# A four-layer graph network on one core: upper target classes in pairs of source blocks, and a third tile picked from SBUF in layer 2

## The chip, the cores and the metric

The kernel runs on one core of one Trainium2 chip. The metric is the device time of one execution in microseconds; before the change it is 7265.93 us, the median of three runs from 7258.8 to 7266.82. Five engines work side by side, each with its own instruction queue: TensorE (PE) multiplies matrices, VectorE (DVE) and ScalarE (ACT) do elementwise work, GpSimd (POOL) here mostly issues gathers, and SyncE (SP) issues most plain transfers. TensorE's weight loads are a row of their own, PEld. SBUF is the working memory of 128 partitions, PSUM holds what TensorE writes, and DRAM holds inputs, outputs and the tables between layers.

## The reference, cut to what matters

There are 12500 nodes with 128 features and 200000 edges, each with a source and a target (src, dst). Targets are sorted and crowd at low numbers: dst is 12500 u^2 for a uniform u. Each of four layers normalizes the nodes, computes messages along the edges, sums them at nodes, and adds the result to x. Layer 0 is a graph attention and layer 1 an attention with eight heads. The two layers that the change concerns most are these, cut to their sums:

```python
# layer 2: every edge counts in both directions
row = concat([src, dst]); col = concat([dst, src])
deg = segment_sum(ones, row) + 1;  dinv = rsqrt(deg)
xw = h @ W
y = segment_sum(dinv[row] * dinv[col] * xw[col], row) + dinv**2 * xw + b
# layer 3: the sums go to the targets only
neigh_sum = segment_sum(feature[src], dst);  deg = segment_sum(1, dst)
h = feature @ W_self.T + neigh_sum / max(deg, 1) @ W_neigh.T + b   # then batch norm, relu, residual
```

So layer 2 needs two kinds of sums: at each edge's source, of rows that belong to its target, and at each edge's target, of rows that belong to its source. Layer 3 needs the second kind only.

## The kernel before, in words

Nodes are held in 98 blocks (NB) of 128 lanes. In layer 0's background the edges are sorted by source block and, inside a block, by target; that order serves layers 1 to 3.

**Sums at the sources (sum_rows, layer 2).** The sorted edges are laid out in 16 tiles (TB) of 128 edges for each source block, and 56 more tiles hold what does not fit. For each tile a gather (an indirect DMA from POOL, line 355) fetches the 128 rows of the edges' targets from the table zt, a 0/1 matrix (hot) says which lane each edge belongs to, and two matmuls (a row is stored as two halves of 16 bits, PARTS) add the rows up in PSUM (line 1988). Four tiles are a group; there are 406 groups, and a row buffer holds a group, in six buffers. As edges of a block are sorted by target, the first tile of a block only points to targets 0 to 127, and the second to 18 to 273. These two are not gathered in blocks 0 to 96: the rows of WINDOWS lie in SBUF (near_rows), the edges' targets are loaded (targets, line 1948), a compare makes a 0/1 matrix of them (line 1951), three matmuls pick the rows (line 1956), and ACT copies them into the row buffer (line 1958). Layer 1 does the same for its own table with the same WINDOWS. The choice depends on the data, so a test made with the lists (source_tiles) sets a flag, and a slow path that gathers everything stands behind it.

**Sums at the targets (buckets, layers 2 and 3).** Targets are cut into 32 classes (CLASSES): 16 (FEW) below target 4864 (SPLIT), 20 to 500 targets wide, and 16 above, 480 wide each. A bucket is one class and one source block; it has room for 128 edges, and a flag (over) sends the work to a slow path if one holds more. A pass handles four classes (AT_ONCE), and goes over all 98 blocks. A load brings two blocks of rows (z, line 962) and their buckets' lane numbers (lanes, line 964, 256 KB, spread to all partitions); DVE compares the lanes (mine, line 968, 512 wide); then, two buckets at a time, which is called a step here, PE reads each bucket's rows out of the block (pout, line 975), DVE makes a 0/1 matrix of places in the class (yours, line 977), ACT copies what was read to SBUF (r, line 980), and PE adds it to the class's sums (line 951, two matmuls per bucket). Layer 2 has 8 passes (all classes); layer 3 has 4, since it sums targets from SPLIT on by late gathers (late_sums).

**What sets the order.** In layer 2, sum_rows walks through the 406 groups and takes steps of the buckets between them; bucket_shares gives each step a cost by its columns, so that a group gets its share of the steps and the two end together. When four classes are done, finish and layer2_out work off the blocks that are complete and store their rows for layer 3 (h). The framework's scheduler then places the instructions; SP's queue is one, and its loads wait in it for their buffers in order. z and lanes have three buffers each, mine two, yours four, pout two.

**The lists of buckets (bucket_starts).** In layer 1's background, written by hand into its order (manual_schedule), the beginnings of all buckets are found: the 3136 keys in 25 columns of 128 (BC) are compared with the first edge of every row of edges (125 compares of 320, line 855), and two gathers per column (bedge) fetch the row that a bucket begins in and then the 128 edges from there. From these come the lanes and the places in the class, stored to DRAM.

Of the kernel before, what the change touches and what calls it, by code (L numbers as in the profile page):

```python
# [79 lines left out]
CLASSES = 2 * FEW  # L80
CURVE, BEND, STEEP, FLAT = 20, 13, 494, 480


def bound(k):

    if k < BEND:
        return CURVE * k * k
    return CURVE * BEND ** 2 + STEEP * (k - BEND) if k < FEW else SPLIT + FLAT * (k - FEW)
# [9 lines left out]
BUCKETS = NB * CLASSES  # L98
BC = -(-BUCKETS // P)
# [5 lines left out]
NEAR, LOW = 2, 18  # L105
WINDOWS = ((0, 0), (1, LOW + P), (1, LOW))

# [25 lines left out]
class Net:  # L133
# [674 lines left out]
    def bucket_starts(self, work, take, keys, firsts, shifted, lanes, places, over):  # L808
# [8 lines left out]
        nc.vector.tensor_scalar(k, k, CLASSES - 1, None, op0=OP.bitwise_and)  # L817
# [3 lines left out]
        k, low, mid, top = (work.tile([P, 2], F32, name=f"bb{i}") for i in range(4))  # L821
# [3 lines left out]
        nc.vector.tensor_scalar(top, k, float(FLAT), float(SPLIT - FLAT * FEW), op0=OP.mult, op1=OP.add)  # L825
        nc.vector.tensor_sub(top, top, mid)
        nc.vector.tensor_sub(mid, mid, low)
        nc.vector.scalar_tensor_tensor(mid, k, BEND - 0.5, mid, op0=OP.is_ge, op1=OP.mult)
        nc.vector.scalar_tensor_tensor(top, k, FEW - 0.5, top, op0=OP.is_ge, op1=OP.mult)
        nc.vector.tensor_add(bound, low, mid)  # L830
        nc.vector.tensor_add(bound, bound, top)
        yield
        cols = work.tile([P, 2], I32, name="bcols")
        nc.vector.tensor_copy(cols, bound)
        nc.vector.tensor_scalar(cols, cols, 7, KEY_BITS, op0=OP.logical_shift_left, op1=OP.bitwise_or)
        head = work.tile([P, 1], F32, name="bhead")
        nc.vector.tensor_scalar(head, bound[:, 0:1], -1.0, 1.0, op0=OP.mult, op1=OP.add)
        least, above = (work.tile([P, BC], I32, name=n) for n in ("bleast", "babove"))
        nc.gpsimd.iota(least, pattern=[[P, BC]], base=0, channel_multiplier=1)
        nc.vector.tensor_scalar(least, least, int(math.log2(CLASSES)), 21, op0=OP.logical_shift_right,  # L840
                                op1=OP.logical_shift_left)
        for i, t in ((1, above), (0, least)):
            nc.vector.tensor_tensor(t, least, cols[:, i:i + 1].to_broadcast([P, BC]), op=OP.bitwise_or)
# [4 lines left out]
        counts = work.tile([P, BC, 5], F32, name="bcounts")  # L848
        for h in range(5):
            f = work.tile([P, quarter], F32, name="bfirst", bufs=2)  # L850
# [79 lines left out]
    def bucket_shares(self, passes):  # L930

        costs = []
        for k0 in passes:
            for s in range(NB):
                costs += [PARTS * (2 * D + sum(WIDE[k0 + i:k0 + i + 2])) + 6 * P for i in range(0, AT_ONCE, 2)]
# [1612 lines left out]
```

## Time and profile before

| | |
|---|---|
| median of three runs | 7265.93 us |
| time of the profiled execution | 7251.91 us |
| its span, first to last instruction | 7250.1 us |
| gathers of layer 0 (hw), first to last | 195.5 to 2162.3 us, 1564 of them |
| gathers of layer 1 (kvt), first to last | 2355.1 to 4243.6 us, 1430, and 50 for the buckets' lists |
| gathers of layer 2 (zt), first to last | 4523.7 to 6338.1 us, 1430 |
| late gathers of layer 3 (h) | 6375.9 to 7169.4 us, 596 |
| mean granted TensorE clock | 0.801 |

The layers follow one another, so that each is read as a stage of its own: in a stage, the engine that never waits is the one that sets the end, and the busy share of an engine over the whole span says little. In the lines of the profile, L355 is line 355 of the kernel; out<-in names what an instruction writes and reads; x is a count. A wait is idle time of an engine, with what ended it; "issue" means that nothing in the profile was waited for. A matmul's duration includes its way through the array, and successive matmuls overlap, so what one costs in a row of them is the distance of two starts.

### The profile page before, as it was taken

The numbers are of one execution on the slowest core, as the hardware profiler recorded it, in microseconds if no ns is written. First come the engines' busy times: TensorE is split into PE (matmuls) and PEld (weight loads), VectorE is DVE, ScalarE is ACT, GpSimd is POOL, SyncE is SP. The second block draws the span as 40 slices with busy tenths as digits, with TensorE's granted clock in tenths as the row PEclk, the third lists the DMA queues.
The fourth block names the chain that finished last, engine by engine and source line by source line (L and its number), as shares of the span: only waits on it lengthen the run. The fifth ranks groups of instructions, "written<-read, shape, count | busy, mean of one in ns | idle before, by whom it ended". The sixth has DMA issues, their size and how long they took to land. (4 is left out here: it accounts for less than half of the span.)

```text
span 7250.1 us, 126419 instructions
## 1 busy us (share of the span) xinstructions
PE 5117.9 (71%) x37041; PEld 4050.0 (56%) x37042; DVE 5586.9 (77%) x17921; ACT 3831.6 (53%) x8238; POOL 5039.5 (70%) x5200
## 2 busy tenths in 40 slices
PE   4344544444446777777777753999999998889987
PEld 3334444444433777666677743555565567745675
DVE  5596777777756888767777757888888888988988
ACT  4466666666656443333333326455555556845567
POOL 0777777777762777777777743777777777767774
PEclk7556666666668777777777756999999999989999
DMA  6433333333346766666666641555555555744565
GB/s 109 90 81 81 83 81 82 81 80 82 82 91 198 222 203 205 191 189 194 189 201 197 201 114 51 132 138 137 140 140 137 136 148 161 196 123 121 140 169 160
DMA packets 808143, 1007.00 MB, mean 139 GB/s; under 512 B 201589, under 2 KB 549882, under 8 KB 807162
## 3 DMA queue, kind: packets, MB, share of 16 engines
q1 hardware_dynamic: 578655, 551.06, 26.6%
q0 software_dynamic: 186016, 432.15, 23.4%
q10 hardware_dynamic: 42747, 15.32, 1.0%
q8 instruction: 309, 5.06, 0.3%
q14 instruction: 416, 3.41, 0.2%
HBM read 937.24 MB, written 60.78 MB: 138 GB/s over the span
## 5 line engine op out<-in xcount | busy, mean ns | idle before, releaser
L355 POOL DMA_INDIRECT rows<-hw,idxd x1564 | 1488.8, 952 | 672.9 <-issue 449.6
L980 ACT ACTIVATE r<-pout 128x512 f16<-128x512 f32 x2352 | 1373.3, 596 | 977.8 <-PE pout L975 909.2
L951 PE MATMUL sums<-yours,r 128*128 128x480 f16 (+9 forms) x9408 | 1863.8, 318 | 4.5 <-ACT r L980 3.7
L355 POOL DMA_INDIRECT rows<-zt,idxs x1430 | 1379.8, 965 | 453.3 <-issue 332.6
L355 POOL DMA_INDIRECT rows<-kvt,idxs x1430 | 1390.0, 972 | 435.8 <-issue 348.0
L977 DVE TENSOR_SCALAR yours<-iotac,bucketp 128x480 f16<-128x480 f16 (+8 forms) x4704 | 1356.9, 336 | 207.0 <-PE sums L951 184.8
L1408 PE MATMUL psum<-rows,weights 128*128 128x130 f32 x3128 | 742.4, 418 | 636.2 <-ACT weights L1402 528.2
L951 PEld LDWEIGHTS <-r 128*128 128x128 f16 x9408 | 861.6, 98 | 374.2 <-issue 11.0
L1408 PEld LDWEIGHTS psum<-rows,weights 128*128 128x128 f32 x3128 | 665.5, 314 | 676.1 <-ACT weights L1402 599.4
L975 PE MATMUL pout<-z,mine 128*128 128x256 f16 x4704 | 893.5, 273 | 49.1 <-ACT r L980 26.7
L355 POOL DMA_INDIRECT rows<-h,late x596 | 585.2, 982 | 182.5 <-issue 142.6
L1687 ACT ACTIVATE weighted<-lg 128x64 f32<-128x64 f32 x203 | 53.1, 262 | 1163.0 <-DVE lg L1685 1163.0
L1402 ACT ACTIVATE weights<-off,weight,minus 128x128 f32<-128x128 bf16 x1173 | 483.3, 481 | 334.7 <-DVE minus L1392 187.0
L975 PEld LDWEIGHTS <-mine 128*128 128x128 f16 x4704 | 431.3, 97 | 325.7 <-issue 72.8
L1708 PE MATMUL psum<-weighted,hot 128*128 128x137 f32 x3136 | 557.8, 347 | 64.8 <-DVE weighted L1697 64.4
L1708 PEld LDWEIGHTS psum<-weighted,hot 128*128 128x128 f32 x3136 | 530.3, 252 | 81.8 <-DVE weighted L1697 76.7
L1681 DVE TENSOR_TENSOR rows<-pq,rows 128x512 f32<-128x512 f32 x406 | 278.7, 687 | 307.3 <-DMA rows<-kvt,idxs 306.2
L1668 PE MATMUL pq<-query,mine 128*128 128x128 f16 x3136 | 296.7, 270 | 262.2 <-DVE mine L1637 239.5
L1661 PE MATMUL pb<-we,near 128*128 128x16 f32 x3248 | 448.3, 281 | 9.7 <-ACT near L1630 9.7
L1661 PEld LDWEIGHTS pb<-we,near 128*128 128x128 f32 x3248 | 441.3, 218 | 22.1 <-ACT near L1630 11.4
L968 DVE TENSOR_SCALAR mine<-lanes,lane 128x512 f16<-128x512 f16 x1176 | 426.4, 365 | 17.4 <-PE pout L975 15.6
L1668 PEld LDWEIGHTS <-mine 128*128 128x128 f16 x3248 | 274.3, 127 | 288.4 <-DVE mine L1637 263.1
(525 smaller groups left out, 9074.7 us busy)
## 6 DMA issues: line engine op xcount, KB each, us to landing
lanes<-lanes SPq DMA_DIRECT2D x588, 256.0 KB
near<-lengths SPq DMA_DIRECT2D x203, 512.0 KB
lanes<-slanest SPq DMA_DIRECT2D x203, 256.0 KB
z<-zt SPq DMA_DIRECT2D x392, 128.0 KB
lanes<-dlanes SPq DMA_DIRECT2D x195, 256.0 KB
z<-h SPq DMA_DIRECT2D x196, 128.0 KB
rows<-hw,idxd POOLq DMA_INDIRECT x1564
rows<-kvt,idxs POOLq DMA_INDIRECT x1430
```

The source lines that it names most:

```text
L355: self.nc.gpsimd.indirect_dma_start(out=out, out_offset=None, in_=table, in_offset=bass.IndirectOffsetOnAxis(ap=idx[:, t:t + 1], axis=0))
L951: nc.tensor.matmul(sums[i], self.part(r[:, i, :], h), yours[i], start=s == NB - 1 and h == 0, stop=s == 0 and h == PARTS - 1)
L968: nc.vector.tensor_scalar(mine, lane[:, s - first, :], self.lane, None, op0=OP.is_equal)
L975: nc.tensor.matmul(p[:, j, :], mine[:, (i + j) * P:(i + j + 1) * P], z[:, s - first, :], start=True, stop=True)
L977: nc.vector.tensor_scalar(yours[j], self.iotac[:, :wide[i + j]], place[:, b:b + 1], None, op0=OP.is_equal)
L980: nc.scalar.activation(r, p, AF.Copy)
L1402: nc.scalar.activation(hot[:, j, :], off, AF.Relu, bias=w[:, j:j + 1], scale=minus[:, j:j + 1])
L1408: nc.tensor.matmul(p, hot[:, j, :], rows[:, j, :n], start=j % G == 0, stop=j % G == G - 1)
L1661: nc.tensor.matmul(pb[:, j].rearrange("p a h -> p (a h)"), s["near"][:, j * P:(j + 1) * P], self.we.rearrange("p a h -> p (a h)"), start=F ...
L1668: nc.tensor.matmul(pq[:, j, :], s["mine"][i][:, j, :], s["query"][i * G + j][:, h * D:(h + 1) * D], start=h == 0, stop=h == 1)
L1681: nc.vector.tensor_mul(k, s["pq"][i], k)
L1708: nc.tensor.matmul(p, s["hot"][j // G][:, j % G, :], v[:, j, :], start=first and j == 0, stop=last and j == W - 1)
```

## The change

**Classes.** Below SPLIT everything stays. Above it there are 20 classes (MANY) instead of 16, from 308 targets wide to 460, and a bucket there holds the edges of *two* source blocks, 64 lanes (HALF) for each. A pass over upper classes goes over 49 pairs; each load of z brings a pair, its lanes are half as large, and a bucket is read by two matmuls of 64 lanes, each writing half of the partitions. There are five upper passes and four lower ones. z and lanes have two buffers each instead of three.

**Lists.** The keys now are 13 columns of lower buckets and 2 x 8 of the upper ones' halves (SC = 29 for the counting, BC = 21 of buckets), and the edges of an upper column are fetched by two gathers of 64. The compares have one buffer (bfirst) instead of two.

**Third tile.** The third tile's targets are expected from 100 to 611 (NEXT, MORE); its rows are picked by four matmuls, with the compare made against the lane and against the lane plus 256 (further), in a second pout tile and a second copy. This is for layer 2 alone: layer 1 still picks two tiles. source_tiles subtracts 100 from the third tile's targets as it does 18 from the second's, and tests its range.

```diff
-CLASSES = 2 * FEW
-CURVE, BEND, STEEP, FLAT = 20, 13, 494, 480
+MANY = 20
+CLASSES = FEW + MANY
+CURVE, BEND, STEEP = 20, 13, 494
+RISE, SPREAD = 304, 4
 def bound(k):
...
+    return SPLIT + (RISE + SPREAD * (k - FEW)) * (k - FEW)
...
-BUCKETS = NB * CLASSES
-BC = -(-BUCKETS // P)
+HALF = P // 2
+LC = -(-NB * FEW // P)
+TC = -(-NB // 2 * MANY // P)
+SC = LC + 2 * TC
+BC = LC + TC
...
-NEAR, LOW = 2, 18
+NEAR, LOW, NEXT = 2, 18, 100
 WINDOWS = ((0, 0), (1, LOW + P), (1, LOW))
+MORE = ((2, NEXT + P), (2, NEXT), (2, NEXT + 3 * P), (2, NEXT + 2 * P))
...
 def bucket_starts
...
-            f = work.tile([P, quarter], F32, name="bfirst", bufs=2)
+            f = work.tile([P, quarter], F32, name="bfirst")
...
-            for c in range(BC):
+            for c in range(SC):
...
+        def parts(c):
+            if c < LC:
+                return [(slice(0, P), c)]
+            return [(slice(h * HALF, h * HALF + HALF), c + h * TC) for h in range(2)]
+
+        def run(c):
             if c < BC:
                 edges[c] = work.tile([P, P], I32, name="bedge", bufs=4)
-                self.gather(edges[c], table, ri, c)
+                for at, col in parts(c):
+                    self.gather(edges[c][:, at], shifted, ri, col)
...
 def bucket_shares
...
+            two = [sum(WIDE[k0 + i:k0 + i + 2]) for i in range(0, AT_ONCE, 2)]
+            if k0 < FEW:
+                costs += [PARTS * (2 * D + w) + 6 * P for w in two] * NB
+            else:
+                costs += [PARTS * (4 * D + w) + 6 * P for w in two] * (NB // 2)
...
 def buckets
...
-            for s in range(NB - 1, -1, -1):
-                first = s // ZB * ZB
-                if s == first + ZB - 1:
-                    z = work.tile([P, ZB, PARTS * D], STORED, name="z", bufs=3)
+            pairs = k0 >= FEW
+            count = NB // 2 if pairs else NB
+            for s in range(count - 1, -1, -1):
+                first = 2 * s if pairs else s // ZB * ZB
+                if pairs or s == first + ZB - 1:
+                    z = work.tile([P, ZB, PARTS * D], STORED, name="z", bufs=2)
                     nc.sync.dma_start(z, view[:, first:first + ZB, :])
-                    lane = work.tile([P, ZB, n * P], F16, name="lanes", bufs=3)
+                    lane = work.tile([P, ZB, n * P], F16, name="lanes", bufs=2)
+                    if pairs:
+                        at, m = (LC * P + s * MANY + k0 - FEW) * P, n * P
+                    else:
+                        at, m = (k0 // n * (LC * P // FEW) + first) * n * P, ZB * n * P
...
+                        if pairs:
+                            b = LC * P + s * MANY + k0 - FEW + i + j
+                            for h in range(2):
+                                at = slice(h * HALF, h * HALF + HALF)
+                                nc.tensor.matmul(p[at, j, :], mine[:, (i + j) * P + h * HALF:(i + j) * P + (h + 1) * HALF],
+                                                 z[:, h, :], start=True, stop=True)
...
 def sum_rows
...
+        spans = WINDOWS + MORE
+        near_rows = work.tile([P, len(spans), PARTS * D], STORED, name="nearrows")
+        for w, (_, lo) in enumerate(spans):
             nc.sync.dma_start(near_rows[:, w, :], table[lo:lo + P, :])
+        further = work.tile([P, 1], F32, name="further")
+        nc.vector.tensor_scalar_add(further, self.lane, 2.0 * P)
...
+            targets = work.tile([P, 5, P], F16, name="targets")
+            nc.sync.dma_start(targets.rearrange("p w e -> p (w e)"), self.targets_of(tile, 5))
+            chosen = work.tile([P, len(spans), P], F16, name="chosen")
+            nc.vector.tensor_scalar(chosen[:, :5], targets, self.lane, None, op0=OP.is_equal)
+            nc.vector.tensor_scalar(chosen[:, 5:], targets[:, 3:], further, None, op0=OP.is_equal)
+            for tiles in ((0, 1), (2,)):
+                p = psum.tile([P, 2, PARTS * D], F32, name="pout", bufs=2)[:, :len(tiles)]
+                for j, tile in enumerate(tiles):
+                    terms = [w for w, (t, _) in enumerate(spans) if t == tile]
+                    for w in terms:
+                        nc.tensor.matmul(p[:, j, :], chosen[:, w, :], near_rows[:, w, :], start=w == terms[0],
+                                         stop=w == terms[-1])
+                nc.scalar.activation(rows[:, tiles[0]:tiles[-1] + 1, :], p, AF.Copy)
...
-            for j in range(NEAR if close else 0, G):
+            for j in range(3 if close else 0, G):
                 self.gather(rows[:, j, :], table, idx, lo + j)
```

## The prediction

> **What bounds the kernel now.** I read the span by stages first, then what each stage's engines wait for, then a stretch of single instructions. The busy time of each engine in four stretches, each taken from the first gather of a layer to its last (layers 0, 1, 2, 3; the columns after the length are busy us and instructions of PE, weight loads, DVE, ACT, POOL, then clock and DMA):
>
> ```profile
> 195.00:2163.00 1968.00, 892.23 (x5386) 807.60 (x5386) 1416.22 (x3348) 1179.51 (x2917) 1488.64 (x1564) 0.62 0.37 83
> 2355.00:4245.00 1890.00, 1420.87 (x10757) 1347.28 (x10757) 1430.47 (x3727) 718.12 (x1531) 1438.85 (x1481) 0.76 0.65 198
> 4523.00:6340.00 1817.00, 1699.29 (x13154) 1120.54 (x13155) 1540.13 (x6247) 1025.74 (x1831) 1379.77 (x1430) 0.99 0.55 148
> 6370.00:7172.00 802.00, 725.40 (x5966) 504.14 (x5967) 725.77 (x2880) 494.69 (x901) 615.82 (x621) 0.98 0.55 150
> ```
>
> By busy share PE (94%) looks like the limit of layer 2 and POOL (76%) does not. The waits of POOL in layer 2 say otherwise (total us, times, longest us):
>
> ```profile
> POOL rows L355 <- issue: 332.6, 1091, 0.3
> POOL rows L355 <- PE pout L975: 32.0, 105, 0.3
> POOL rows L355 <- DMA rows<-zt,idxs: 22.9, 75, 0.3
> POOL rows L355 <- PE sums L951: 21.0, 69, 0.3
> POOL rows L355 <- DVE hot L1986: 17.7, 1, 17.7
> POOL rows L355 <- PE psum L1988: 13.7, 45, 0.3
> ```
>
> Every wait but the first of the stage is 0.3 us, whoever is named: it is the fixed gap before each gather, not a wait for anybody. The timeline shows the beat, 3.98, 5.23, 6.48:
>
> ```profile
> 5003.98 0.94 POOL L355 DMA_INDIRECT rows<-zt,idxs  x1 [0.30 <-issue]
> 5004.17 0.38 PE L975 MATMUL pout<-z,mine 128*128 128x256 f16 x2
> ...
> 5004.38 0.97 PE L951 MATMUL sums<-yours,r 128*128 128x480 f16 x4
> ...
> 5005.19 0.38 PE L975 MATMUL pout<-z,mine 128*128 128x256 f16 x2
> 5005.23 0.94 POOL L355 DMA_INDIRECT rows<-zt,idxs  x1 [0.30 <-issue]
> ...
> 5005.41 0.97 PE L951 MATMUL sums<-yours,r 128*128 128x480 f16 x4
> ...
> 5006.48 0.94 POOL L355 DMA_INDIRECT rows<-zt,idxs  x1 [0.30 <-PE sums L951]
> ```
>
> So layer 2 is bound by POOL: 1430 gathers from 4523.7 to 6338.1 are 1.270 us each. Layer 1 is too: 1480 gathers (50 of them bedge) from 2355.1 to 4243.6, 1.277 us each. PE is a close second in layer 2. Its step in the upper classes (two bucket reads and four sums) takes 1.02 us when nothing interrupts it (5004.17 to 5005.19 above): four sums of 480 columns at a pitch of 0.20, two reads of 256 columns at 0.11.
>
> **The change, part by part.**
>
> *Third tile (close_rows).* Of the 16 tiles of each of 97 blocks, 14 were gathered and now 13: 97 gathers less, 97 x 1.270 = 123 us off the engine that sets the stage. Added per block: four matmuls of 256 columns (0.11 each by pitch), an eviction of 256 columns (between the 0.27 of the 64-wide and the 0.60 of the 512-wide ACT copy; I take 0.45), one longer and one additional DVE compare (the present 384-wide one takes 0.34; I take 0.42 and 0.30). That is 43 us of PE, 44 of ACT and 37 of DVE, all beside the gathers.
>
> *Upper classes by pairs of blocks.* The steps (two buckets each) go from 8 x 98 x 2 = 1568 to 4 x 98 x 2 + 5 x 49 x 2 = 1274, the upper ones from 784 to 490. An upper step keeps four sums, of 384 columns on average (0.20 x 384/480 = 0.16 each), and has four reads of 64 lanes instead of two of 128. No row shows such a read. Bounds: 0.055 if the two halves run side by side, 0.27 (the whole duration of a read in its row) if each must leave the array before the next enters. I take 0.11, the pitch of the present read, as each half streams the same 256 columns. Step: 4 x 0.16 + 4 x 0.11 = 1.08. PE in the upper classes: 784 x 1.02 = 800 to 490 x 1.08 = 529 us. DVE loses 147 lane compares at 0.365 and 588 of the 1568 compares of 480 columns that take 508.8 us, the others getting narrower (0.30): about 54 + 215 us; ACT loses 294 x 0.596 = 175.
>
> Sum for the stage by engine: PE 1699 - 271 + 43 = 1471, DVE about 1310, ACT 900, POOL's beat 1333 x 1.270 = 1693. POOL stays the bound and PE's cover grows from 7% to 13%. The work per gather group also fits locally: by the planner's costs a group gets 8840 units instead of 11000, so 2.66 upper steps in 1333/406 x 1.27 = 4.17 us. PE needs 2.66 x 1.08 = 2.87, plus 0.65 for eight hot matmuls (pitches of 0.05 to 0.11) and 7 x 0.11/4 = 0.19 for the close ones: 3.7. What is late next is therefore still the gathered rows.
>
> *Mode of the array.* The 64-lane reads use a part of the array, the sums the whole, and they alternate. Layer 0 has such a change already, a 64-column matmul between 128-column ones:
>
> ```profile
> 592.25 0.39 PE L1408 MATMUL psum<-rows,weights 128*128 128x130 f32 x2
> 592.47 0.27 PE L524 MATMUL bank<-ident,keys 128*64 128x128 f32 x1
> 592.58 0.39 PE L1408 MATMUL psum<-rows,weights 128*128 128x130 f32 x2
> ```
>
> Starts 592.25, (592.36), 592.47, 592.58: the same 0.11 pitch into it and out of it, no bubble. [...]
>
> *Bucket lists, in the background of layer 1.* Gathers of edges: 25 + 25 become 29 + 13 + 2 x 8 = 58. Eight more on a bound POOL: 8 x 1.277 = +10 us. (Bounds: 0 if the odd longer intervals of that stage absorb them, 10 if not; the intervals are tight, so 10.) Counting compares 125 to 145 at 0.54 + 0.08: 12 us of DVE, which idles 459 of 1890 us there; the stores of lanes and places go on SP, idle between loads. bfirst has one buffer instead of two, so four times DVE (and behind it that iteration's logits) waits for a 160 KB load, some 3 us. Ten row buffers of four gathers, 50 us of POOL's beat, cover that; without cover 4 x 3 = 12 us.
>
> *Buffers.* z and lanes go from three buffers to two in layers 2 and 3. On SP a z load waits for PE's last read of the old buffer and the lanes load behind it in the queue waits with it. In the trace's DMA records the last packet of a lanes load (256 KB) lands 3.3 us (median) after its issue; before the change it lies 8 to 9 us early in the wide passes, 2.2 us early in the last pass of either layer. With two buffers a load is issued one buffer's time later: 5.2 us in the wide passes (covered), 2.6 in the last one of layer 3, so there about 0.2 to 0.6 us late for 49 loads, +8 to +29; I take 8. In the upper passes of layer 2 a buffer lasts two steps of 4.17/2.66 = 1.57 us, and z has two steps and the sums of a third, 4.3 us, from release to use against some 2.9 (issue 0.37, and z packets that land 1.7 to 2.5 after it); PE's 11% cover stands behind that.
>
> *Small edits.* Four more near-row loads at 0.42 on SP ahead of the first z load and four short DVE operations where the source lists are made: +3.
>
> **Sum** against the profiled execution, 7251.9: -123 + 10 + 8 + 3 = -102, so 7150. That execution is 14 us under the median of the three runs, 7265.9; carried over to the median: **7164 us**.
>
> **Rivals.**
> 1. *PE takes over in the upper classes, but gives back only part.* From a read of (4.17 - 0.84)/2.66 = 1.25, (1.25 - 0.64)/4 = 0.153 us, PE is later than the rows. At 0.18 a group takes 4.45 us, 184 groups lose 53: 7217. For: nearly full PE now, unknown 64-lane reads. Against: the 0.11 pitch at 592.47.
> 2. *The slower one: the half reads serialize.* From 0.207 us a read the 102 us are used up. At 0.27 (fill and stream of each exposed) a step is 1.72, a group 5.42, 184 groups lose 230: 7395. For: weights of 64 lanes just before each read, halves of one bank. Against: the same row in layer 0, and weight loads now overlap (0.10 beside a 0.11 pitch).
> 3. *Late z and lanes.* Were each of the 245 upper loads 0.3 us late beyond PE's cover and layer 3's 196 too: 441 x 0.3 = 132 us, 7296; limited to layer 3 and half of it, 7195. For: SP is one queue in order, and a late z holds the lanes behind it. Against: the 4.3 us above.
> 4. *The guarded fallbacks run*, thousands of us, if a half bucket holds 64 edges or more or a third tile leaves its window. Counted in the inputs: the fullest half holds 62, third tiles reach from 146 to 557 inside 100 to 611. Excluded.
>
> **How the numbers follow.** Forecast 0.69; rival 1 0.10; rival 3 0.07 (of it 0.02 within noise, 0.01 slower); rival 2 0.14, of it 0.01 within noise. A measurement of this kernel tells 0.2%, 15 us, from no change. Faster 0.69 + 0.10 + 0.04 = 0.83, same 0.03, slower 0.14 (rivals 2 and 3). The forecast's own range is 7116 (no new costs and the 20 ns above the 1.25 beat gone) to 7195. To leave out no more than 2 in 10 it goes on to rival 1's end: 7115 to 7255.
>
> **What would show it.** Right: 1333 gathers of zt at 1.26 to 1.28 us, longest wait 0.3; layer 2 about 1690 us from first to last gather; PE waiting for rows more than the 74 us now; 58 bedge gathers and layer 1 10 us longer; layer 3 up to 10 longer. Wrong: POOL waits above 0.3 us for psum or pout (rival 1 and 2), a 64-lane read with a pitch above 0.15, PE waits for z, DVE for lanes (rival 3), or a granted clock in layer 2 under the 0.99 of now because PE pauses more.

## The result, and the profile after

The changed kernel takes 7175.2 us (median of 4 runs, 7168.2 to 7180.5) where the kernel before takes 7266.2 (4 runs, 7258.8 to 7266.8): ratio 0.9876, 95% interval 0.9859 to 0.9894. It is faster by 1.2%. The prediction said 7164, in a range from 7115 to 7255.

The profiled execution took 7176.9 us (span 7175.1), that of before 7251.9 (span 7250.1). The traces therefore differ by 75 us and the medians by 91; the traced execution of before was 14 us under its median, the one of after 2 us over. What follows accounts for the 75.

The same view by stages as before, first gather to last of layers 0, 1, 2, and the gathers and last pass of layer 3 (length, then busy us and instructions of PE, weight loads, DVE, ACT, POOL, then clock and DMA):

```profile
196.10:2160.80 1964.70, 884.77 (x5385) 801.47 (x5386) 1417.18 (x3348) 1177.66 (x2912) 1485.67 (x1563) 0.62 0.37 83
2346.20:4249.40 1903.20, 1417.72 (x10748) 1344.51 (x10749) 1441.84 (x3780) 717.22 (x1527) 1450.38 (x1490) 0.75 0.65 197
4531.80:6228.80 1697.00, 1500.84 (x12634) 942.79 (x12635) 1317.84 (x5563) 882.74 (x1623) 1289.23 (x1333) 0.98 0.58 149
6276.40:7102.40 826.00, 734.50 (x6036) 508.49 (x6037) 728.17 (x2915) 499.63 (x907) 619.63 (x619) 0.98 0.54 144
```

Layer 2 went from 1814.4 us (4523.7 to 6338.1) to 1697.0, and every engine in it lost work: PE 1699 to 1501, DVE 1540 to 1318, ACT 1026 to 883. Which of these losses is the gain can't be read here. The waits in layer 2 tell more:

```profile
POOL rows L363 <- issue: 322.7, 1053, 2.0
...
PE psum L2057 <- DMA rows<-zt,idxs: 121.8, 145, 2.7
...
POOL rows L363 <- DMA rows<-zt,idxs: 21.9, 72, 0.3
...
POOL rows L363 <- DVE hot L2055: 17.7, 1, 17.7
POOL rows L363 <- PE sums L999: 14.6, 48, 0.3
...
PE pout L1031 <- DMA z<-zt: 13.6, 12, 2.3
```

The gather (L363 now) is still separated from the next by its fixed 0.3 us. Of the 1332 gaps between two gathers of this layer one is longer, a pause of 2.0 us behind the first gather; before the change none of the 1429 was over 0.32 us. So in both traces layer 2 is, from its first gather to its last, gathers and their fixed gaps with nothing else between them. PE waits longer for gathered rows than before, where the line was

```profile
PE psum L1988 <- DMA rows<-zt,idxs: 73.8, 91, 2.3
```

The rows are late, not PE. The beat is visible in the timeline (5.19, 6.44, 7.68) beside an upper step, which begins with four reads of 64 lanes:

```profile
5005.19 0.95 POOL L363 DMA_INDIRECT rows<-zt,idxs  x1 [0.30 <-issue]
...
5005.94 0.41 PE L1031 MATMUL pout<-z,mine 128*64 128x256 f16 x4
...
5006.28 0.81 PE L999 MATMUL sums<-yours,r 128*128 128x372 f16 x4
...
5006.44 0.94 POOL L363 DMA_INDIRECT rows<-zt,idxs  x1 [0.30 <-issue]
...
5007.02 0.41 PE L1031 MATMUL pout<-z,mine 128*64 128x256 f16 x4
...
5007.68 1.08 POOL L363 DMA_INDIRECT rows<-zt,idxs  x1 [0.30 <-issue]
```

The step takes 1.08 us (5005.94 to 5007.02), the number the prediction had worked out.

Where the 75 us of the two traces lie, stage by stage:

| stretch | before | after | difference | predicted |
|---|---|---|---|---|
| start and layer 0, with the stretch to layer 1 | | | -8.9 | +3 (small edits, here or later) |
| layer 1, first gather to last | 1888.5 | 1903.2 | +14.7 | +10 |
| layer 1 to layer 2 | | | +2.3 | 0 |
| layer 2, first gather to last | 1814.4 | 1697.0 | -117.4 | -123 |
| last gather of layer 2 to layer 3 | 39.5 | 49.5 | +10.0 | 0 |
| four passes of layer 3 | 800.8 | 824.1 | +23.3 | +8 |
| end | | | +1.0 | 0 |
| sum | | | -75.0 | -102 |

The passes of layer 3 went from 267.2, 234.8, 171.8, 127.0 us to 271.7, 236.2, 172.8, 143.4: most of the loss is in the last pass. Its waits in the trace of after name what is late:

```profile
DVE mine L1021 <- DMA lanes<-lanes: 14.0, 26, 1.3
...
PE pout L1035 <- DMA z<-h: 4.8, 6, 2.1
```

Before the change, VectorE never waited for lanes in layer 3, and TensorE never for z. The last 200 us of layer 2 (mostly its last pass of lower classes) show the same two waits:

```profile
PE pout L1035 <- DMA z<-zt: 11.3, 9, 2.1
...
DVE mine L1021 <- DMA lanes<-lanes: 4.6, 6, 1.1
```

Before the change each came once there:

```profile
PE pout L975 <- DMA z<-zt: 1.0, 1, 1.0
...
DVE mine L968 <- DMA lanes<-lanes: 0.2, 1, 0.2
```

This pass took 128 us for its 196 steps before and 157 after. Most of that is not these waits: 110 gathers lie in the pass instead of 92, as the planner spreads the steps over the groups anew, and 18 beats are 23 us. The last eviction of classes came 9.1 us after the last gather before, with 14 steps still to do at that gather, and 18.2 us after, with 26 steps to do: most of the +10 at the end of layer 2.

### The profile page after: what moved, and what is told of

Its sections match the earlier page's. It is cut to its first block, busy times and chain, and to the rows that moved or that the text cites. A ratio compares the mean times of both kernels' runs of the same rounds, so it can differ in the third digit from the quotient of the medians.

```text
span 7175.1 us, 124612 instructions
## 1 busy us (share of the span) xinstructions
PE 4924.0 (69%) x36641; PEld 3872.9 (54%) x36642; DVE 5389.6 (75%) x17358; ACT 3695.0 (51%) x8043; POOL 4965.4 (69%) x5112
## 5 line engine op out<-in xcount | busy, mean ns | idle before, releaser
L363 POOL DMA_INDIRECT rows<-hw,idxd x1564 | 1486.6, 951 | 673.7 <-issue 448.6
L1040 ACT ACTIVATE r<-pout 128x512 f16<-128x512 f32 x2058 | 1200.6, 596 | 1049.9 <-PE pout L1035 604.0
L363 POOL DMA_INDIRECT rows<-kvt,idxs x1430 | 1394.0, 975 | 435.6 <-issue 357.3
L363 POOL DMA_INDIRECT rows<-zt,idxs x1333 | 1290.2, 968 | 425.4 <-issue 322.7
L999 PE MATMUL sums<-yours,r 128*128 128x494 f16 (+20 forms) x8232 | 1517.8, 304 | 5.9 <-ACT r L1040 4.1
L1037 DVE TENSOR_SCALAR yours<-iotac,bucketp 128x494 f16<-128x494 f16 (+26 forms) x4116 | 1137.4, 325 | 259.4 <-PE sums L999 240.9
L999 PEld LDWEIGHTS <-r 128*128 128x128 f16 x8232 | 712.7, 98 | 354.1 <-issue 106.2
L363 POOL DMA_INDIRECT rows<-h,late x596 | 590.8, 991 | 190.0 <-issue 140.5
L1035 PE MATMUL pout<-z,mine 128*128 128x256 f16 x3136 | 597.4, 275 | 78.9 <-ACT r L1040 28.2
L1733 PEld LDWEIGHTS <-mine 128*128 128x128 f16 x3248 | 269.5, 125 | 329.1 <-DVE mine L1702 248.2
L2057 PE MATMUL psum<-rows,hot 128*128 128x128 f16 x3248 | 311.2, 220 | 170.6 <-DMA rows<-zt,idxs 121.8
L1035 PEld LDWEIGHTS <-mine 128*128 128x128 f16 x3136 | 279.4, 97 | 238.5 <-issue 59.7
```

The costliest lines, as they stand in the source:

```text
L363: self.nc.gpsimd.indirect_dma_start(out=out, out_offset=None, in_=table, in_offset=bass.IndirectOffsetOnAxis(ap=idx[:, t:t + 1], axis=0))
L999: nc.tensor.matmul(sums[i], self.part(r[:, i, :], h), yours[i], start=start and h == 0, stop=stop and h == PARTS - 1)
L1035: nc.tensor.matmul(p[:, j, :], mine[:, (i + j) * P:(i + j + 1) * P], z[:, s - first, :], start=True, stop=True)
L1037: nc.vector.tensor_scalar(yours[j], self.iotac[:, :wide[i + j]], place[:, b:b + 1], None, op0=OP.is_equal)
L1040: nc.scalar.activation(r, p, AF.Copy)
L1733: nc.tensor.matmul(pq[:, j, :], s["mine"][i][:, j, :], s["query"][i * G + j][:, h * D:(h + 1) * D], start=h == 0, stop=h == 1)
```

## Theories, and the chips they were tried on

**Theory A**, the prediction's: POOL's gathers come at a fixed beat of 1.27 us and set layer 2; 97 of them fewer is the gain, and TensorE only has to stay under the beat. **Theory B**, its rival: TensorE, 94% busy, was the limit, and the classes in pairs relieved it. Two further questions are what the change of the array's mode costs, and whether two buffers instead of three make the losses in layer 3 and at the end of layer 2.

Of the twelve runs, one (the reads issued twice) was on a chip on which the kernel before took 7276 us. On the chips of all the others it took 9121 to 9277 us, so their totals are told as ratios to the kernel before on the same chip. On these chips every engine pauses often (in 14 us of the pairs-only kernel's first run, 5649 to 5663, TensorE idles up to 2.5 us at once, VectorE 2.8, ScalarE 5.8, POOL 1.2), and nothing in the trace says for what. Single instructions of VectorE, ScalarE and POOL last as long as elsewhere (in layer 2 a mean of 238, 541 and 970 ns in the kernel of experiment 4 with three buffers in layer 3, against 237, 544 and 967 in the changed kernel; the 512-column eviction 596 ns in both), and gathers arrive as quickly: from the issue to the last packet a median of 2.45 us in layer 2 of the pairs-only kernel, 2.9 in the changed kernel's trace. But the fixed 0.3 us before a gather is no longer the longest wait. The waits of POOL in layer 2 of the pairs-only kernel (second run):

```profile
POOL rows L363 <- issue: 476.7, 1192, 5.6
POOL rows L363 <- PE psum L2054: 116.2, 58, 5.2
```

TensorE is slower in the mean: in layer 2 of the changed kernel with three buffers in layer 3 (experiment 4) a full bucket read takes 304 ns against 276 (median 272 in both), the granted clock is 0.86 against 0.98, and PE is busy 1701 us instead of 1501 with the same matmuls. Whether the lower clock follows from the pauses or adds to them is not shown. The names of the releasers mean little there, as most records of semaphores are missing from these traces (the pairs-only kernel's second has 1,800 to 2,800 of some 9,800 for each of eight semaphores that DMA landings set). What makes the pauses stays open. These chips answer questions about the array's pitches, and what the parts are worth when engines pause; they do not answer what the parts are worth by themselves on the chip of the prediction.

## Experiment 1: more work for TensorE alone

```
                             for h in range(2):
                                 at = slice(h * HALF, h * HALF + HALF)
+                                for _ in range(2):
-                                nc.tensor.matmul(p[at, j, :], mine[...], z[:, h, :], start=True, stop=True)
+                                    nc.tensor.matmul(p[at, j, :], mine[...], z[:, h, :], start=True, stop=True)
```

> The changed kernel with every 64-lane read issued twice (the second overwrites the first with the same values): 490 steps x 4 reads more, at 0.05 to 0.13 us each some 100 to 250 us of TensorE in layer 2, which did 1501 us of work there beside 1333 gathers x 1.27 = 1697. Theory A (the beat of the gathers sets layer 2): the first 200 us of it cost nothing, layer 2 stays at 1697 to 1745 us, gathers at 1.25 to 1.31, total within 45 us of the changed kernel's on the same chip (7175 where the kernel before takes 7266). Theory B (TensorE sets layer 2): the whole 100 to 250 us is added, layer 2 1800 to 1950.

Measured: 7204.1 us beside 7276.2 of the kernel before (one run each). The changed kernel's ratio would put it at 7186 on that chip, so 18 us were added. Layer 2 took 1718.6 us (4540.5 to 6259.1), 21.6 more than in the changed kernel. What TensorE got to do, from the timeline:

```profile
5004.86 0.63 PE L1032 MATMUL pout<-z,mine 128*64 128x256 f16 x8
...
5005.43 0.81 PE L999 MATMUL sums<-yours,r 128*128 128x372 f16 x4
...
5006.17 0.63 PE L1032 MATMUL pout<-z,mine 128*64 128x256 f16 x8
```

A step from 5004.86 to 6.17 is 1.31 us; over 111 steps that nothing interrupted the median is 1.30, against 1.08 in the changed kernel. So TensorE got 490 x 0.22 = 108 us more, and layer 2 got a fifth of that longer. Theory B asked for all of it.

The fifth is where POOL had to wait: its gaps beyond the fixed 0.3 us add up to 23.7 us in layer 2, against 2.0 in the changed kernel, and the difference of 21.7 is the whole lengthening. The same 400 us inside the upper classes, in the kernel before, in the changed kernel and with the reads issued twice (PE busy first after the length):

```profile
4900.00:5300.00 400.00, 381.79 (x2705) 235.73 (x2704) 328.47 (x1260) 206.91 (x362) 303.36 (x318) 1.00 0.52 138
```

```profile
4900.00:5300.00 400.00, 365.47 (x3169) 202.37 (x3167) 301.40 (x1259) 197.81 (x364) 303.73 (x316) 0.99 0.62 155
```

```profile
4900.00:5300.00 400.00, 394.88 (x4021) 244.66 (x4018) 292.33 (x1186) 188.17 (x346) 291.55 (x304) 1.00 0.60 148
```

TensorE is busy 95%, 91% and 99% of the time. From TensorE's first read of an upper bucket to its last, the gathers are 1.2661, 1.2658 and 1.2985 us apart in the mean. Between 95 and 91% the beat does not move; at 99% it does. Whole passes of four classes say the same: before the change TensorE is busy 89 to 96% in them and the beat is 1.264 to 1.279 us, after it 80 to 93% and 1.265 to 1.286. So on chips without pauses the beat set layer 2 before and after, and the pairs did not shorten it. With the reads issued twice TensorE takes over in the upper classes alone: there the gathers lie (1.2985 - 1.2658) x 620 = 20 us later in all.

## Experiment 2: the parts alone

Pairs alone, the third tile gathered again:

```
-        spans = WINDOWS + MORE
+        spans = WINDOWS
...
-            for tiles in ((0, 1), (2,)):
+            for tiles in ((0, 1),):
...
-            for j in range(3 if close else 0, G):
+            for j in range(2 if close else 0, G):
```

> The changed kernel, but the third tile of each block is gathered again (two tiles are picked by TensorE, as in the kernel before); the upper classes stay in pairs. Theory A (the beat of the gathers sets layer 2, TensorE only has to stay under it): 1430 gathers at 1.270 to 1.274 us, layer 2 1816 to 1822 us from first to last gather, the total 117 to 124 us over the changed kernel's 7175: 7292 to 7299, slower than the kernel before by 0.3 to 0.5%, although TensorE is relieved by some 200 us. Theory B (TensorE was the bound of layer 2 and the pairs relieved it): layer 2 within 20 us of the changed kernel's 1697, total 7155 to 7195.

> The kernel of the pairs-only run again, now that the kernel before takes 7276 us and not 9121. Theory A (the beat of the gathers sets layer 2): 1430 gathers at 1.270 to 1.274 us, layer 2 1816 to 1822, total 117 to 124 us over the changed kernel's 7175: 7292 to 7299, 0.3 to 0.5% slower than the kernel before. Theory B (TensorE sets it): layer 2 within 20 us of 1697, total 7155 to 7195.

The same with the memory as it was before the change (z and lanes with three buffers in both layers, the firsts of the lists with two; a scratch tile is shared to make room):

```
-                    z = work.tile([P, ZB, PARTS * D], STORED, name="z", bufs=2)
+                    z = work.tile([P, ZB, PARTS * D], STORED, name="z", bufs=3)
...
-                    lane = work.tile([P, ZB, n * P], F16, name="lanes", bufs=2)
+                    lane = work.tile([P, ZB, n * P], F16, name="lanes", bufs=3)
...
-            f = work.tile([P, quarter], F32, name="bfirst")
+            f = work.tile([P, quarter], F32, name="bfirst", bufs=2)
```

> The pairs alone, with the memory of the kernel before: two tiles are picked and 14 gathered, z and lanes have three buffers in both layers, the firsts of the lists two. Numbers for a chip on which the kernel before takes 7266. Theory A (the gathers' beat sets layer 2): 1430 gathers at 1.270, layer 2 1816 to 1820 us; layer 1 +10 for 8 gathers, its 4 to 5 us for the load of the firsts gone; the last classes copy 9 us after the last gather (18 with two buffers); the passes of layer 3 at 267, 235, 172, 127. Total 7266 + 10 + 3 = 7279, range 7265 to 7295: no gain although TensorE is relieved by 15% in layer 2. Theory B (TensorE's relief makes the gain): layer 2 1697 to 1750, total 7150 to 7210. Rival on the buffers: layer 3 stays at 272, 236, 173, 143 and the tail at 18, for a reason other than buffers: 25 us more. Where the kernel before takes some 9120 us (the other chips): as the pairs-only run, 9061, less up to 36.

> The kernel of the run before (pairs alone, the memory of the kernel before) once more, for a chip without the pauses. There, with the kernel before at 7266: theory A: 1430 gathers at 1.270, layer 2 1816 to 1820 us, total 7265 to 7295, so no gain from the pairs by themselves; passes of layer 3 at 267, 235, 172, 127 if buffers were the cause of 272, 236, 173, 143. Theory B: layer 2 1697 to 1750, total 7150 to 7210. If the chip has the pauses again (the kernel before at 9100 to 9300): ratio 0.986 to 0.991 as measured, and the question of the pairs alone stays open for a chip without them.

The third tile alone, put into the kernel before. The masks share the two `mine` tiles, and z has two buffers in layer 2:

```
-    for j in range(NEAR if close else 0, G):
+    for j in range(3 if close else 0, G):
...
-    z = work.tile([P, ZB, PARTS * D], STORED, name="z", bufs=3)
+    z = work.tile([P, ZB, PARTS * D], STORED, name="z", bufs=deep[0])      # layer 2: 2, layer 3: 3
```

> The kernel before with the pick of the third tile alone: 32 classes, one bucket per block as before; z and lanes have two buffers in layer 2 (three do not fit beside the near rows) and three in layer 3. TensorE then has 1699 + 43 = 1742 us of work in layer 2 against 1333 gathers x 1.27 = 1693. Theory A with a close second (the later of the two sets the stage): layer 2 takes 1742 to 1790 us, the gathers show waits over 0.3 us for pout or psum, total 7190 to 7240. If the gathers alone count, whatever TensorE does: layer 2 1693 to 1700, total 7266 - 117 = 7149 or less, and the pairs were not needed. Theory B (TensorE alone is the bound): layer 2 1817 + 43 = 1860, total about 7309.

> The kernel of the third-tile-only run again, same reason. TensorE has 1699 + 43 = 1742 us of work in layer 2 against 1333 gathers x 1.27 = 1693. Theory A with a close second: layer 2 1742 to 1790 us, waits of the gathers over 0.3 us, total 7190 to 7240. If the gathers alone count: layer 2 1693 to 1700, total 7149 or less, and the pairs were not needed. Theory B: layer 2 about 1860, total 7309.

The changed kernel with the third tile gathered as well, into a buffer that nobody reads:

```
                 close_rows(rows, lo)
+                spare = work.tile([P, PARTS * D], STORED, name="spare", bufs=2)
+                self.gather(spare, table, idx, lo + 2)
```

> The changed kernel with TensorE's pick of the third tile, but that tile gathered as well, into a spare buffer that nobody reads: TensorE, VectorE and ScalarE do all that they do in the changed kernel, and POOL has its 1430 gathers again. Theory A: layer 2 1816 to 1822 us, total 7292 to 7299, as with the pairs only. Rival (the removed work of the other engines or of the waits for gathered rows makes the gain, not the 97 beats): layer 2 1697 to 1740, total 7175 to 7215.

Measured, all on chips with the pauses (the two values are two chips; layer 2 from first gather to last; the last column adds up POOL's gaps between gathers of layer 2 as far as they go beyond the fixed 0.3 us):

| kernel | ratio to the kernel before, 95% interval | layer 2, us | POOL's pauses, us |
|---|---|---|---|
| pairs alone, two buffers | 0.9931 (0.9911 to 0.9951), 0.9927 (0.9900 to 0.9953) | 2329, 2315 | 498, 478 |
| pairs alone, three buffers | 0.9884 (0.9857 to 0.9911), 0.9914 (0.9887 to 0.9941) | 2349, 2319 | 514, 492 |
| third tile alone | 1.0014 (0.9998 to 1.0030), 1.0005 (0.9986 to 1.0024) | 2423, 2409 | 716, 701 |
| both, and the third tile gathered too | 1.0031 (1.0017 to 1.0045) | 2398 | 571 |
| both, three buffers in layer 3 (experiment 4) | 0.9925 (0.9909 to 0.9940) | 2292 | 594 |

Layer 2 of the last two rows differs by the 97 gathers that nobody reads, and by the chip (the kernel before takes 9124 us on the one and 9121 on the other). The windows of the two, with the additional gathers first:

```profile
5583.40:7981.80 2398.40, 1713.37 (x12585) 1031.40 (x12586) 1326.12 (x5539) 874.35 (x1615) 1391.53 (x1430) 0.85 0.41 108
```

```profile
5578.20:7870.50 2292.30, 1701.37 (x12567) 1030.26 (x12568) 1319.53 (x5534) 872.10 (x1613) 1292.55 (x1332) 0.86 0.41 110
```

PE, DVE and ACT do the same in both (1713 and 1701, 1326 and 1320, 874 and 872 us), POOL has 97 gathers more, and layer 2 is 106 us longer: 1.09 us for a gather that nobody waits for. Theory A had said 117 to 124 for a chip without pauses. So a gather costs its time even here, and the rival that the gain comes from waits for the rows falls. Whether it costs as POOL's turn alone or also as a transfer, this run can't tell apart.

What theory A does not say is that the work put in its place costs nearly as much on these chips. The last column shows where. Without the pauses layer 2 is 1.27 to 1.29 us for each gather in every row, as on the chip of the prediction; the pauses come on top, and they grow with the work of the other engines. With the pick they are 594 us instead of 478 to 514, and without the pairs 701 to 716 instead of 594: the pick adds some 100 us of them, and the pairs take some 100 away. Taking the pick away from that kernel and leaving the gathers (pairs alone, two buffers) makes layer 2 shorter by 70 to 83 us, so the change gains only 23 to 36 us of its 106. The third tile alone gains nothing within the interval, where theory A asked for 0.4 to 1.6% on a chip without pauses. The pairs alone gain 0.7 to 1.2%, where theory A asked for none. With pauses on every engine none of them seems to set the time by itself: layer 2 takes 1.72 us for each gather instead of 1.27, and TensorE is busy 1701 of its 2292 us. So here the work that the pairs save on TensorE, VectorE and ScalarE counts, in the direction of theory B, though TensorE is no full engine either.

For the chip of the prediction the split between the parts is therefore not shown by a run of the parts. It rests on the two traces and experiment 1: the beat is 1.2697 us over 1430 gathers before and 1.2740 over 1333 after, with one pause in 2761 gaps, and in the upper classes it did not move with TensorE's load between 91 and 95%. Whether the third tile could have been taken there without the relief of the pairs stays open.

## Experiment 3: the mode of the array

```
-                                at = slice(h * HALF, h * HALF + HALF)
-                                nc.tensor.matmul(p[at, j, :], mine[:, (i + j) * P + h * HALF:(i + j) * P + (h + 1) * HALF],
-                                                 z[:, h, :], start=True, stop=True)
+                                nc.tensor.matmul(p[:, j, :], mine[:, (i + j) * P:(i + j + 1) * P],
+                                                 z[:, h, :], start=h == 0, stop=h == 1)
```

> The changed kernel, but an upper step reads its two buckets with four matmuls over all 128 lanes (both source blocks through the whole weight tile, the second added to the first) in place of four half ones of 64 lanes: the array keeps one mode. What it computes for the upper classes is therefore not the reference's sum. In the changed kernel's trace the two halves of a pair start 3 ns apart, pairs 0.13 us; a first read starts 0.26 us after a sum, a sum 0.205 after a read. Theory (a change of mode costs some 0.1 us each way): a read follows a sum after 0.16 to 0.17 us, a sum a read after 0.11, the four reads take 4 x 0.11; step 4 x 0.16 + 4 x 0.11 = 1.08, as now, because side by side halves had paid for the two changes. Rival (the gaps come from the weights or the data of these reads, not from the mode): 0.26 and 0.205 stay, the step is 0.2 longer. Total in both cases as the changed kernel's (7175 +- 15), since TensorE stays 0.1 us or more per gather under the gathers.

The chip was one with the pauses (9069.6 us; the kernel before 9141.3), so the total says nothing about the 7175; the pitches inside a step can be read where nothing interrupts it. The timeline of this kernel:

```profile
6081.15 0.80 PE L999 MATMUL sums<-yours,r 128*128 128x372 f16 x4
6081.79 0.60 PE L1030 MATMUL pout<-z,mine 128*128 128x256 f16 x4
6082.22 0.83 PE L999 MATMUL sums<-yours,r 128*128 128x388 f16 x4
```

Medians of the time from one matmul's start to the next in the upper classes:

| from, to | 64-lane reads | 128-lane reads |
|---|---|---|
| hot matmul, first read | 0.149 us | 0.055 |
| sum, first read | 0.258 | 0.187 (upper quarter disturbed; lower quarter 0.160) |
| first half, second half of a bucket | 0.003 | 0.109 |
| first bucket, second bucket | 0.130 | 0.109 |
| last read, sum | 0.205 | 0.109 |

Going into the 64-lane reads costs 0.149 - 0.055 = 0.094 us, coming out 0.205 - 0.109 = 0.096. In return the two halves of a bucket run side by side: they start 3 ns apart and last 289 ns each in the mean. From the first read to the first sum it is 0.003 + 0.130 + 0.003 + 0.205 = 0.34 us, and with 0.09 for going in 0.43; four full reads take 4 x 0.109 = 0.44. The theory of the expectation holds: the change of mode is paid for by the overlap, and the step is the same either way. Between its two buckets the step loses 0.02 us more (0.130 against 0.109). Experiment 1 agrees: there two more pairs of half reads, with no change of mode between them, lengthened the step by 0.22 us, 0.11 for a pair, so the gaps of 0.09 to 0.10 are not a cost of each narrow read.

## Experiment 4: the buffers

Three buffers for z and lanes in layer 3 alone, and then in addition three for z in layer 2 and two for the firsts of the lists (the edit of experiment 2, with the third tile picked):

```
-    def buckets(self, work, psum, table, lanes, place, finish, passes):
+    def buckets(self, work, psum, table, lanes, place, finish, passes, deep=(2, 2)):
...
-    self.buckets(work, psum, ht_, lanes, place, finish, passes)
+    self.buckets(work, psum, ht_, lanes, place, finish, passes, deep=(3, 3))
```

> The changed kernel with three buffers for z and lanes in layer 3 alone (two in layer 2). If the two buffers are the whole loss in layer 3: its passes return to 267, 235, 172 and 127 us (now 272, 236, 173, 143), VectorE's waits for lanes to 0, total 7175 - 16 to - 23 = 7152 to 7159. Rival (the lanes of lower classes now lie in rows 16 instead of 32 classes long, or the transfers of layer 3 are slower for another reason): passes as now, total 7170 to 7180.

> The changed kernel with three buffers for z and lanes in layer 3, three for z in layer 2 (lanes two), and two again for the firsts of the bucket lists in layer 1 (bfirst; a scratch tile is shared to make room). Theory: layer 3 -16 to -23; the last classes copy of layer 2 comes 9 us after the last gather instead of 18, -9, if the wait for z makes that tail (0 if it is the split of the steps over the gathers); layer 1's 14.7 us fall to 10.2 (8 gathers x 1.275), -4, if the wait for bfirst makes the rest. Sum 7175 - 16 to - 36: 7139 to 7159. Rival: only layer 3 moves, as in the run with three buffers there.

> The kernel with the buffers back (layer 3: z and lanes three; layer 2: z three; bfirst two) again, same reason. Layer 3's passes back to 267, 235, 172 and 127 us, -16 to -23; last classes copy of layer 2 9 us after the last gather instead of 18, -9 (0 if the split of the steps makes that tail); layer 1's gathers from 14.7 us over the kernel before to 10, -4. Sum 7139 to 7159. Rival: the buffers are not the cause and the passes stay at 272, 236, 173, 143.

Measured, on chips with the pauses: 0.9925 (0.9909 to 0.9940) for layer 3 alone; 0.9889 (0.9869 to 0.9909) and 0.9882 (0.9852 to 0.9913) for all three. The passes of layer 3 are 327, 295, 217, 191 us with three buffers and 327, 285, 222, 192 with two (pairs alone): no difference. The last eviction of classes comes 23 to 28 us after the last gather with two and with three. On these chips the work on a load lasts longer (49 loads in the 191 us of the last pass are 3.9 us each, against 2.6 where nothing pauses; in layer 2 of the trace of before a lanes load landed 3.3 us after its issue, the median), which may be why the buffers can't be told there, and the 0.4% between the two versions has no stage to which it belongs: layer 1 is 8 to 11 us shorter with two buffers for the firsts in this pair, but not in the runs of the pairs alone.

So the experiment was inconclusive. That two buffers make the 23 us of layer 3 is argued from the new waits in the changed kernel's trace, which add up to 18.8 us there, 16.8 of them in its last pass, and were 0 before the change. For the 10 us before it the waits (15.9 us in the last 200 us of layer 2; 1.2 before) stand beside a rival, the planner's new split of the steps over the gathers, and no run tells the two apart. Whether the version with the buffers back beats the changed kernel on the chip of the prediction stays open; against the kernel before, on the other chips, it is the fastest of those tried, by 1.1 to 1.2%, level with the pairs alone with three buffers.

## Why the prediction was right, and where it was not

- **What bounds layer 2: right.** The waits of 0.3 us were read as the beat, and 1430 gathers at 1.2697 became 1333 at 1.2740. That is 117.4 us instead of 123. Of the missing 6, the 0.0043 us that each of 1333 gathers is later make all: 1.7 us are the one new pause, and 4.0 are the gather instructions, 967.9 ns in the mean instead of 964.9. What makes them longer is open.
- **Third tile "all beside the gathers": right on this chip, with the pairs' relief in place.** PE 1501 us against the 1471 worked out, DVE 1318 against 1310, ACT 883 against 900, all under 1697. It is not right on a chip with pauses, where that work cost 70 to 83 us.
- **Upper step 1.08 us: the number was right and its reason wrong.** The prediction took each half read at the 0.11 of a full one and no cost for the mode, by the fp32 row of layer 0. In truth the halves overlap (its own lower bound; they start 3 ns apart) and the mode costs 0.094 us in and 0.096 out, 0.19 per step, 0.19 x 490 = 93 us of PE. The two errors cancel to 0.43 against 0.44. Why the fp32 row shows no cost stays open; its 0.11 on the way out is the shortest of the 22 such matmuls of layer 0, five of which have 0.37, for the mode or for their inputs. The 30 us that PE is over the 1471 were not followed further.
- **Rival 1, its threshold: the size was right.** It said that from a step of 1.25 us TensorE is late. Experiment 1 put the step at 1.30; by the same working 2.66 x 1.30 + 0.84 = 4.30 us per group instead of 4.17, over 184 groups 24 us. Measured: 20 in the upper classes, 21.6 in layer 2.
- **"Buffers ... I take 8": mis-sized.** The bounds were 8 to 29 in layer 3, and 23 came; the lower end was taken without a row that favoured it. The place was right, the last pass of layer 3. That the last pass of layer 2 has the same short steps was named in the 2.2 us of slack but not in the sum, which has nothing for the end of layer 2; the +10 came there, from these waits or from the new split of the steps. The upper passes, for which rival 3 feared the most, waited for z 12 times, 13.6 us in all, and PE's cover held.
- **"Bucket lists +10": 14.7, and the cover held.** Eight gathers are 10.2. DVE waited four times, up to 4.1 us, 15.2 in all, for the load of the firsts; the prediction had 12 as the cost without cover and counted it as covered. It was: no gap between two gathers of layer 1 is over 0.35 us in either trace, so these waits did not reach POOL. The remaining 4.5 us are the gather instructions themselves, 975.1 ns in the mean over 1488 of them instead of 972.1, the same 3 ns as in layer 2.
- **What it said the profile would show.** Right: 1333 gathers between 1.26 and 1.28 us, layer 2 near 1690 (1697.0), PE's wait for rows above 74 (121.8). Wrong: a longest wait of 0.3 (2.0), and layer 3 up to 10 us longer (23). Of its signs of error three appeared. TensorE's waits for z and VectorE's for lanes are rival 3, at the price that it gave for half of layer 3 or less, and without deciding. The granted clock of layer 2 is 0.98 instead of 0.99, with PE idle for some 196 us of it instead of 118; under a beat that POOL sets this cost nothing that can be seen.
- **The sum.** By the traces -75 instead of -102: 15 for layer 3, 10 for the end of layer 2, 6 for the beat, 5 for layer 1, and 3 in the gaps between stages, against some 12 by which the start, layer 0 and the way to layer 1 fell short of the +3 of the small edits. The change doesn't explain these: in the trace of experiment 1, whose program is the same up to layer 2, layer 1 starts at 2354.9 us, where it started before the change (2355.1), and not at 2346.2. By the medians it is -91, as the traced execution of before was a quick one. That the median came within 11 us of the forecast is therefore partly luck: 12 us from the start and 16 from how the traced executions lie to their medians make up for much of what the sum missed.

## What to carry to other kernels

Ask of a stage what its slowest regular instruction waits for. Here POOL's beat with its fixed gap of 0.3 us set the time of layer 2 at a busy share of 76%, and TensorE, busy 95% beside it, was still covered: the beat moved only at 99%. When a change takes a buffer to make room, look for the shortest steps that use it, in each stage, and price the late load there at the middle of its bounds, not at the lower one (here 23 us came of bounds of 8 to 29). And compare what a part is worth on more than one chip before calling it the gain: the same removed gather was worth 1.09 us where engines pause, but the work put in its place cost 0.7 to 0.9 there. Where they don't pause, layer 2 kept 117 of the 123 us, with the relief of the pairs beside it.

## What the runs showed of the hardware that was not expected

- Two 64-column fp16 matmuls on the two halves of the array start 3 ns apart, and changing between them and full ones costs 0.094 us in and 0.096 us out (the changed kernel against experiment 3). A 64-column weight load takes 109 ns in the mean, one of 128 columns 97 to 99.
- The same program took 25 to 28% longer on most of the chips. The instructions of VectorE, ScalarE and POOL took as long as elsewhere (a mean of 238, 541 and 970 ns in layer 2 against 237, 544 and 967), matmuls longer in the mean (a full read 304 ns against 276, at a granted clock of 0.86 against 0.98 in layer 2), with pauses of 2 to 6 us between them (TensorE 2.5, VectorE 2.8, ScalarE 5.8, POOL 5.6 in the pairs-only kernels), and repeated runs on two such chips agreed within 0.1% for the pairs, the third tile and the buffers (9061.5 and 9061.4, 9129.4 and 9129.7, 9025.6 and 9023.7 us).
- On those chips a gather that nobody reads still cost 1.09 us of layer 2, and POOL's pauses grew with the work of the other engines, from 478 to 716 us in layer 2.
